# Spreading the d_all transfers over four slots, one product behind the second scan, and a Silu read from PSUM, in a Mamba-then-attention kernel

## The chip, the cores and the metric

The kernel runs on one core of one Trainium2 chip. The metric is device time in microseconds (us) for the whole program, as the median of several runs; three runs of the kernel before gave 7906.63, 7911.72 and 7912.80 us. The trace belongs to one further execution.

## What is computed

The input x is 4 images of 512 channels by 64 x 64 points, float32. Two layers follow each other, each added to its input.

- Layer 0: a group norm over 16 channels, then a layer norm over the 512 channels. The channels are cut into 4 chunks of 128, and each chunk goes through the same Mamba mixer over L = 4096 points: a projection to 2 x 256 (xi and a gate z), a causal convolution with 4 taps on xi, Silu on both, a projection to a time step dt and to B and C of 16 states, and the recurrence

```
h[t] = exp(dt[t] * A) * h[t-1] + dt[t] * x[t] * B[t]      # 256 channels x 16 states
y[t] = sum over states of h[t] * C[t]
out  = out_proj((y + D * x) * silu(z)) + skip * input
```

  Another layer norm and a 512 x 512 projection end the layer.
- Layer 1: a group norm and a linear attention (relu on q and k; k and q are summed over all points first, so that the second half is one 512 x 512 matrix applied to every point).

## The kernel before, in words

**Steps and slots.** The points of an image are cut into tiles of T = 512. A *step* is one image, one tile and one chunk: 4 x 8 x 4 = 128 steps, in that order. Within a step the 256 channels are two halves (e = 0, 1), the 16 states four groups of four (q), and the channels of a half four blocks of 32 (j). One instruction then holds 32 channels x 4 states on the 128 partitions. A *slot* is two of the four blocks of one (e, q); a step has SLOTS = 2 x 4 x 2 = 16 slots, e = 0 in slots 0 to 7 and e = 1 in slots 8 to 15. Two slots, an even one and the odd one after it, are a *pair*: they fill one tile h of four blocks (`hs`, 2 buffers).

**What a slot does** (`slot`, L725). VectorE (DVE) runs two scans (L739), each h of one block from a decay dA in PSUM and an input bx. ScalarE (ACT) makes the decays, dA = exp(dt * A) (`decay`, L713), three ahead (LEAD = 3, three PSUM banks), so a decay can be written only when the scan three before it has read its bank. GpSimd (POOL) makes bx = d * B for two blocks at once (`drive`, L721), two slots ahead with three buffers. In an even slot, between its two scans, the finished pair before it is multiplied by C: the first 384 of 512 points on DVE, with C spread over partitions in a PSUM bank (`product`, L759; `c_row` refills that one bank), while POOL did the last 128 points at the end of the odd slot (L751, C from `c_sb`). TensorE (PE) then sums over the states into y (`fold_states`, L763), which frees the h tile.

**What the queues carry.** All DMAs named here are issued by SyncE (SP), in the order of the code. In an even slot `b_row` issues 4 transfers of 64 KB that spread a row of B over partitions (`b_all`, 3 buffers, L688); in an odd slot `c_tail` issues 4 of 16 KB for `c_sb` (2 buffers, L688), for the pair that starts in the next slot and is multiplied at the end of the one after. `d_all` (2 buffers, one for each half) holds dt and dt * x of one half, spread from rows in HBM: `spread` (L633) issues 8 transfers of 256 KB in one go, in slot 1 for the half of slots 8 to 15 of the same step, and in slot 9 for the half of slots 0 to 7 of the next step. The first decay of a half runs in slot 6 or 14, and the first bx too (slot + 2). Every DMA of this program signals on one of eight semaphores, taken in turn, and waits first until the DMA eight before it has landed; this is what the built program of the kernel shows for each DMA.

**Around it.** The order is written out by hand, since the scheduler is off inside the loop (L1095): `after` (L1109) runs at the end of each slot, first what was put off with `later(n, ...)`, then fixed work by slot number s, then pieces of norms, projection and attention from queues (`ahead`, `late`, `rest`, `light`), as far as a credit of matmul work allows. The fixed work that matters here: at slots 3, 5, 6, 7, 8, 9 a piece of `inputs` for two steps ahead (four pieces of convolution, then pz for e = 0 and e = 1, whose PSUM banks are copied into xz one slot later, L608); at slot 3 softplus between two table loads (L1128, L1130); at slot 4 `to_rows`; at slot 10 Silu of the whole xz, 2048 elements (L1049), and a table load back (L1150). AWAY = (3, 10) names those two slots. At slots 1 and 9 POOL also runs `gate` (L781), at slot 4 dt * x (L628).

Of the kernel before, what the change touches and what calls it, by code (L numbers as in the profile page):

```python
# [14 lines left out]
P = 128  # L15
# [9 lines left out]
def kernel(  # L25
# [553 lines left out]
    def inputs(f, xn, c, nm):  # L579

        xz = f["xz"] = wk.tile([P, 2, NH, T], F32, tag="xz", name=f"xz_{nm}", bufs=3)
        pc = [None] * NH

        def taps(e, ks):
            for k in ks:
                mm(
                    pc[e], w_cv[:, k, e * P : (e + 1) * P], xn[:, c, k : k + T],
                    start=(k == 0), stop=(k == NTAP - 1),
                )

        def take(e):
            nc.scalar.activation(xz[:, 0, e, :], pc[e], AF.Identity, bias=cb[:, e : e + 1])

        for e in range(NH):
            pc[e] = work_bank(f"pc_{nm}_{e}", 0)
            taps(e, range(NTAP // 2))
            yield
            taps(e, range(NTAP // 2, NTAP))
            later(1, lambda e=e: take(e))
            yield  # L600
        for e in range(NH):
            pz = work_bank(f"pz_{nm}_{e}", 0)
            mm(
                pz, w_z[:, e * P : (e + 1) * P], xn[:, c, NTAP - 1 : NTAP - 1 + T],
                start=True, stop=True,
            )

            later(1, lambda e=e, pz=pz: nc.scalar.copy(xz[:, 1, e, :], pz))  # L608
            yield

    def time_banks(f, nm):
# [18 lines left out]
        f["d_rows", v] = d_rows  # L630
        later(1, lambda: nc.sync.dma_start(d_rows, both[:, v]))

    def spread(f, e, nm):  # L633

        d = wk.tile([P, 2, NJ, T], F32, tag="d_all", name=f"d_all_{nm}_{e}")
        for v in range(2):
            src = f["d_rows", v].rearrange("(j i) e t -> i e j t", i=BLK)[:, e]
            for k in range(KS):
                nc.sync.dma_start(d[k * BLK : (k + 1) * BLK, v], src)  # L639
        f["d_all", e] = d  # L640

    def mixers(f, nm):

# [81 lines left out]
    def slot(g, last, after):  # L725
        n, e, q, jj = place(g)
        b, t, c = steps[n]
        if g + 2 < last:
            drive(g + 2)
        if jj == 0:  # L730
            if g + 3 * JJ < last:
                b_row(g + 3 * JJ)
            hs[g // JJ] = wk.tile([P, NJ, T], F32, tag="h", name=f"h_{g}", bufs=2)
        elif g + 1 < last:
            c_tail(g + 1)
        h = hs[g // JJ]
        for i in range(2):
            j = jj * 2 + i
            nc.vector.tensor_tensor_scan(  # L739
                h[:, j, :], dAs.pop(2 * g + i), bxs[g][:, i, :],  # L740
                0.0 if t == 0 else st[:, c, e, q, j : j + 1], ALU.mult, ALU.add,
            )
            if 2 * g + i + LEAD < 2 * last:
                decay(2 * g + i + LEAD)
            if i == 0 and jj == 0 and g:
                product(g - 1)
                fold_states(g - 1, last)
        del bxs[g]
        if jj == JJ - 1:
            nc.gpsimd.tensor_copy(st[:, c, e, q, :], h[:, :, T - 1])  # L750
            nc.gpsimd.tensor_tensor(  # L751
                h[:, :, CUT:], h[:, :, CUT:], bc(c_sb.pop(g // JJ), NJ), ALU.mult
            )
        after()
# [291 lines left out]
        return inputs(fs[n], xn[b, t], c, names[n])  # L1046

    def silu(n):
        nc.scalar.activation(fs[n]["xz"], fs[n]["xz"], AF.Silu)  # L1049

    ahead, late, rest, light = [], [], [], []

# [26 lines left out]
    time_steps(fs[0], names[0])  # L1079
    for v in range(2):  # L1080
        to_rows(fs[0], v, names[0])
    spread(fs[0], 0, names[0])
    for g in range(JJ, 3 * JJ, JJ):
        b_row(g)
    c_row(0)
# [9 lines left out]
    with tc.manual_schedule():  # L1095
        credit, seen, mix, held[0], held_x[0] = 0.0, work["mm"], iter(()), 0, 0
        for n, (b, t, c) in enumerate(steps):
            f, nm = fs[n], names[n]
            before = fs[n - 1] if n else None
            nxt = fs[n + 1] if n + 1 < N else None  # L1100
            front = step_inputs(n + 2) if n + 2 < N else iter(())
            last_mix, mix = mix, mixers(fs[n + 2], names[n + 2]) if n + 2 < N else iter(())
            if c == 0 and (t + 1 < NT or b + 1 < B):
                add_to(ahead, tile_norm(b, t + 1) if t + 1 < NT else tile_norm(b + 1, 0))
            if c == 0 and t == 0 and b + 1 < B:
                add_to(light, input_norm(b + 1))
            assert c != 2 or not ahead
            for s in range(SLOTS):
                def after():  # L1109
                    nonlocal credit, seen  # L1110
                    now[0] = n * SLOTS + s
                    for what in [w for at, w in due if at <= now[0]]:
                        what()
                    due[:] = [d for d in due if d[0] > now[0]]
                    if s == 0 and before is not None:
                        take_y(before, n - 1, 1)
                    if s == SLOTS // 2:
                        take_y(f, n, 0)
                    if s < 2:
                        next(last_mix, None)  # L1120
                    if s == 1:
                        spread(f, 1, nm)
                        if before is not None:
                            gate(before, 1)
                    if s == 2 and nxt is not None:
                        time_banks(nxt, names[n + 1])
                    if s == 3 and nxt is not None:
                        nc.scalar.preload_act_table_set("softplus")  # L1128
                        time_steps(nxt, names[n + 1])
                        nc.scalar.preload_act_table_set("natural_log_exp_and_others")  # L1130
                    if s == 6 and before is not None:
                        pb_, pt_, pc_ = steps[n - 1]
                        with_skip(before, xn[pb_, pt_], pc_)
                        if pc_ == NC - 1:
                            add_to(late, leave(pb_, pt_))
                    if s in (3, 5, 6, 7, 8, 9):
                        next(front, None)
                    if s == 4 and nxt is not None:
                        to_rows(nxt, 0, names[n + 1])
                        to_rows(nxt, 1, names[n + 1])  # L1140
                    if s == 4 and before is not None:
                        pb_, pt_, pc_ = steps[n - 1]
                        out_proj(before, xn[pb_, pt_], pc_, names[n - 1])
                    if s == 9:
                        gate(f, 0)
                        if nxt is not None:
                            spread(nxt, 0, names[n + 1])
                    if s == 10 and n + 2 < N:
                        silu(n + 2)
                        nc.scalar.preload_act_table_set("natural_log_exp_and_others")  # L1150
                    if s >= 12:
                        next(mix, None)
                    may = [
                        what for k, what in ((0, "wide"), (1, "one ahead"), (2, "two ahead"))
                        if any(a - 2 * k <= s <= a - k for a in AWAY) or (k == 2 and s == SLOTS - 1)
                    ]
                    if light and light[0][1] == "wait" or s in AWAY and not any(
                        q and q[0][1] == "wide" for q in (ahead, late)
                    ):
                        one(light)  # L1160

                    limit[0] = 1 if 0 < s < 6 else 2
                    credit = min(credit + 3.5 - (work["mm"] - seen), 2.6)
                    busy = False
                    for queue in (ahead, late, rest):
                        kind = queue[0][1] if queue else None
                        if queue is ahead or kind == "free" or credit > 0 or kind == "more" and not busy:
                            start = work["mm"]
                            one(queue, ANYWHERE if queue is ahead and (c, s) > (1, 4) else may)
                            credit -= work["mm"] - start  # L1170
                            busy = busy or work["mm"] - start > 1
                    seen = work["mm"]

                slot(n * SLOTS + s, N * SLOTS, after)
            fs[n - 1].clear() if n else None
        product(N * SLOTS - 1)
        fold_states(N * SLOTS - 1, N * SLOTS)
        now[0] = None
        for _, what in due:
            what()  # L1180
# [60 lines left out]
```

## Time and profile before

| | |
|---|---|
| median of three runs | 7911.72 us |
| the profiled execution | 7900.44 us |
| its span, first to last instruction | 7898.7 us |
| mean granted TensorE clock | 0.901 |
| first scan starts, last scan ends | 123.2 us, 7424.1 us |
| busy: DVE, POOL, PE, ACT | 6908.9, 6894.4, 6434.6, 5509.8 us |
| bytes moved by DMA | 1265.87 MB |

How to read it. In a row of a group, the columns are: line, engine, operation, output<-inputs, partitions x elements of output and input, number; then busy us, mean ns of one; then the engine's idle time just before these instructions, and who ended most of it. In the list of waits a row says which instruction waited for which, us in total, how many times, and the longest. In a timeline a row gives start and length in us, and in brackets the idle time before it with its releaser. SPq is SP's queue: its rows are DMA issues. From 7424 us on only the rest of the last image's attention is left.

### The profile page before, as it was taken

Reading aid. Unit: us, or ns where it says so; the run is one execution under the profiler, and the core shown is the slowest. Engines: PE = TensorE matmul, PEld = TensorE weight load, DVE = VectorE, ACT = ScalarE, POOL = GpSimd, SP = SyncE. Lnnn points to the kernel's source line nnn. Section 1 sums busy time; section 2 is a strip of 40 time slices with the busy share of each in tenths; the row PEclk is TensorE's granted clock in tenths of the full one; section 3 lists DMA queues with packets and bytes.
Section 4 is the critical chain, followed back from the end, with each engine's and each line's share of the span. In section 5 each row is a group of like instructions: output and inputs, shape, how many; then the busy total and the mean of one; then the engine's idle time right before and its main releaser. Section 6 shows DMA issues by size and latency. Waiting matters only on the chain.

```text
span 7898.7 us, 90490 instructions
## 1 busy us (share of the span) xinstructions
PE 6434.6 (81%) x24834; PEld 2109.1 (27%) x24880; DVE 6908.9 (87%) x5650; ACT 5509.8 (70%) x8329; POOL 6894.4 (87%) x4649
## 2 busy tenths in 40 slices
PE   5676777677789888988788888888788888888599
PEld 1121212112223232322222223322122222322144
DVE  5999999999999999989999999998989999988500
ACT  4677777777777777777777777777777777777421
POOL 4999999999999999989999999999999999999500
PEclk7888888788899999999899999999889999999799
DMA  5676666666776666776766666777666666677402
GB/s 156 167 170 168 159 153 158 161 155 165 171 176 165 161 163 159 182 187 174 170 167 169 171 164 159 175 179 181 164 159 169 158 164 155 156 194 182 102 32 91
DMA packets 829184, 1265.87 MB, mean 160 GB/s; under 512 B 183912, under 2 KB 317560, under 8 KB 816384
## 3 DMA queue, kind: packets, MB, share of 16 engines
q1 hardware_dynamic: 804736, 1222.32, 61.5%
q0 software_dynamic: 16896, 33.56, 2.5%
q10 hardware_dynamic: 7040, 4.20, 0.2%
q8 instruction: 195, 3.19, 0.2%
q14 instruction: 317, 2.60, 0.1%
HBM read 1052.78 MB, written 206.57 MB: 159 GB/s over the span
## 4 chain that ended last, share of the span: by engine, by line
DVE 32%; PE 21%; DMA 13%; ACT 12%; issue 8%; POOL 7%; SPq 6%; POOLq 0%; DVEq 0%; ACTq 0%
DVE h L739 22%; DVE h L759 9%; DMA d_all<-d_rows 7%; PE pq L124 5%; POOL bx L721 5%; ACT dA L713 4%; PE pc L124 4%; SPq L688 3%; PE y L124 3%; PE pr L124 2%; SPq L639 2%; PE po L124 2%; DMA c_sb<-c_rows 2%; ACT xz L1049 2%; DMA b_all<-b_rows 2%
## 5 line engine op out<-in xcount | busy, mean ns | idle before, releaser
L721 POOL TENSOR_TENSOR bx<-d_all,b_all 128x1024 f32<-128x1024 f32 x2048 | 4824.4, 2369 | 157.7 <-DVE h L739 141.3
L739 DVE TENSOR_TENSOR_SCAN h<-dA,st,bx 128x512 f32<-128x512 f32 x3584 | 4358.0, 1264 | 372.5 <-ACT dA L713 164.4
L713 ACT ACTIVATE dA<-d_all,a_t 128x512 f32<-128x512 f32 x4096 | 2754.3, 687 | 1501.3 <-DVE h L739 1444.7
L759 DVE TENSOR_TENSOR h<-h,c_all 128x1536 f32<-128x1536 f32 x1024 | 1767.6, 1726 | 0.1
L751 POOL TENSOR_TENSOR h<-h,c_sb 128x512 f32<-128x512 f32 x1024 | 1301.1, 1271 | 227.2 <-DMA c_sb<-c_rows 125.1
L124 PE MATMUL y<-h,fold 128*32 128x512 f32 x8192 | 1271.6, 697 | 93.2 <-POOL h L751 88.6
L124 PE MATMUL c_all<-parts,sel 128*128 128x384 bf16 x1024 | 368.3, 360 | 1073.2 <-DVE h L759 1071.0
L124 PE MATMUL pc<-xn,w_cv 128*128 128x512 f32 x2048 | 1037.4, 640 | 118.7 <-DVE xn L414 63.9
L124 PE MATMUL pq<-w_qk,xa 128*128 128x512 f32 x2048 | 963.8, 604 | 7.8 <-issue 4.9
L739 DVE TENSOR_TENSOR_SCAN h<-dA,bx 128x512 f32<-128x512 f32 x512 | 591.8, 1204 | 88.5 <-ACT dA L713 62.7
L124 PEld LDWEIGHTS <-sel 128*128 128x128 bf16 x1280 | 126.8, 99 | 1716.1 <-DVE h L759 1519.5
L124 PEld LDWEIGHTS pc<-xn,w_cv 128*128 128x128 f32 x2048 | 386.5, 199 | 736.4 <-issue 418.0
L124 PEld LDWEIGHTS pq<-w_qk,xa 128*128 128x128 f32 x2048 | 396.6, 195 | 443.7 <-issue 425.4
L124 PE MATMUL pr<-xb,m 128*128 128x512 f32 x1024 | 481.8, 608 | 12.3 <-DMA xb<-x 7.0
L124 PE MATMUL pp<-xn,w_pr 128*128 128x512 f32 x1024 | 477.9, 597 | 4.8 <-DVE xn L414 4.8
L124 PEld LDWEIGHTS y<-h,fold 128*32 128x32 f32 x8192 | 170.3, 114 | 661.9 <-issue 322.4
L124 PE MATMUL y<-xz,dg 32*32 32x512 f32 x2048 | 335.8, 731 | 0.0
L781 POOL TENSOR_TENSOR xz<-xz 128x512 f32<-128x512 f32 x256 | 325.9, 1273 | 5.9 <-ACT xz L778 5.8
L832 ACT ACTIVATE kq<-pq 128x512 f32<-128x512 f32 x256 | 150.6, 588 | 253.3 <-PE pq L124 252.5
L124 PE MATMUL pd<-xz,w_xp 128*128 128x512 f32 x512 | 318.3, 753 | 7.8 <-ACT xz L1049 7.8
L628 POOL TENSOR_TENSOR dt<-dt,xz 128x1024 f32<-128x1024 f32 x128 | 302.5, 2363 | 22.5 <-ACT dt L620 22.5
L124 PE MATMUL pz<-xn,w_z 128*128 128x512 f32 x512 | 273.2, 625 | 9.7 <-ACT xz L608 8.2
(177 smaller groups left out, 5981.2 us busy)
## 6 DMA issues: line engine op xcount, KB each, us to landing
d_all<-d_rows SPq DMA_DIRECT2D x2048, 256.0 KB, 6.6
b_all<-b_rows SPq DMA_DIRECT2D x4096, 64.0 KB, 2.2
d_rows<-dt SPq DMA_DIRECT2D x256, 512.0 KB, 3.7
c_sb<-c_rows SPq DMA_DIRECT2D x4096, 16.0 KB, 1.8
xs<-in_x_dram SPq DMA_DIRECT2D x32, 1024.0 KB, 6.1
xn<-in_x_dram SPq DMA_DIRECT2D x32, 1024.0 KB, 6.2
xr<-in_x_dram POOLq DMA_DIRECT2D x32, 1024.0 KB, 10.2
x<-xr SPq DMA_DIRECT2D x32, 1024.0 KB, 4.2
```

Of the source, the lines that this page charges most:

```text
L124: nc.tensor.matmul(out_, lhsT, rhs, **how)
L628: nc.gpsimd.tensor_tensor(f["both"][:, 1], f["both"][:, 0], f["xz"][:, 0], ALU.mult)
L639: nc.sync.dma_start(d[k * BLK : (k + 1) * BLK, v], src)
L688: nc.sync.dma_start(dst[k * BLK : (k + 1) * BLK, :], rows_[q * KS + k, :].partition_broadcast(BLK))
L713: nc.scalar.activation(dAs[k], fs[n]["d_all", e][:, 0, j, :], AF.Exp, scale=a_t[:, e, j, q : q + 1])
L721: nc.gpsimd.tensor_tensor(bxs[g], fs[n]["d_all", e][:, 1, jj * 2 : jj * 2 + 2, :], bc(b_all[g // JJ], 2), ALU.mult)
L739: nc.vector.tensor_tensor_scan(h[:, j, :], dAs.pop(2 * g + i), bxs[g][:, i, :], 0.0 if t == 0 else st[:, c, e, q, j : j + 1], ALU.mult, AL ...
L751: nc.gpsimd.tensor_tensor(h[:, :, CUT:], h[:, :, CUT:], bc(c_sb.pop(g // JJ), NJ), ALU.mult)
L759: nc.vector.tensor_tensor(own, own, bc(c_all.pop(g // JJ), NJ), ALU.mult)
L781: nc.gpsimd.tensor_tensor(f["xz"][:, 1, e, :], f["xz"][:, 1, e, :], f["xz"][:, 0, e, :], ALU.mult)
L832: nc.scalar.activation(qk[i], pq, AF.Relu)
L1049: nc.scalar.activation(fs[n]["xz"], fs[n]["xz"], AF.Silu)
```

## The change

Three edits.

1. `spread` takes a part 0 to 3 and issues 2 of the 8 transfers: parts 0 and 1 are the dt half (v = 0), parts 2 and 3 the dt * x half (v = 1). They run in slots 0 to 3 (was: all in slot 1) and 8 to 11 (was: all in slot 9). The d_all tile is taken with part 0, one slot earlier than before. `gate(before, 1)` stays in slot 1.
2. In slot 10 alone, `product` and `fold_states` of the pair before come behind the second scan (and the decay behind it), not between the two scans.
3. The second half of the gate branch is no longer copied from PSUM to xz and then put through Silu with the rest: Silu of slot 10 becomes one instruction of 1536 elements in place, and one of 512 elements from the PSUM bank pz to xz.

```diff
-            later(1, lambda e=e, pz=pz: nc.scalar.copy(xz[:, 1, e, :], pz))
+            if e + 1 < NH:
+                later(1, lambda e=e, pz=pz: nc.scalar.copy(xz[:, 1, e, :], pz))
+            f["pz"] = pz
             yield
...
-    def spread(f, e, nm):
-        d = wk.tile([P, 2, NJ, T], F32, tag="d_all", name=f"d_all_{nm}_{e}")
-        for v in range(2):
-            src = f["d_rows", v].rearrange("(j i) e t -> i e j t", i=BLK)[:, e]
-            for k in range(KS):
-                nc.sync.dma_start(d[k * BLK : (k + 1) * BLK, v], src)
-        f["d_all", e] = d
+    def spread(f, e, nm, part):
+        if part == 0:
+            f["d_all", e] = wk.tile([P, 2, NJ, T], F32, tag="d_all", name=f"d_all_{nm}_{e}")
+        v, half = divmod(part, 2)
+        src = f["d_rows", v].rearrange("(j i) e t -> i e j t", i=BLK)[:, e]
+        for k in range(half * KS // 2, (half + 1) * KS // 2):
+            nc.sync.dma_start(f["d_all", e][k * BLK : (k + 1) * BLK, v], src)
...
-            if i == 0 and jj == 0 and g:
+            if i == int(g % SLOTS == AWAY[1]) and jj == 0 and g:
                 product(g - 1)
                 fold_states(g - 1, last)
...
     def silu(n):
-        nc.scalar.activation(fs[n]["xz"], fs[n]["xz"], AF.Silu)
+        xz = fs[n]["xz"].rearrange("p i e t -> p (i e) t")
+        nc.scalar.activation(xz[:, : 2 * NH - 1], xz[:, : 2 * NH - 1], AF.Silu)
+        nc.scalar.activation(xz[:, 2 * NH - 1], fs[n]["pz"], AF.Silu)
...
-                    if s == 1:
-                        spread(f, 1, nm)
-                        if before is not None:
-                            gate(before, 1)
+                    if s < 4:
+                        spread(f, 1, nm, s)
+                    if s == 1 and before is not None:
+                        gate(before, 1)
...
                     if s == 9:
                         gate(f, 0)
-                        if nxt is not None:
-                            spread(nxt, 0, names[n + 1])
+                    if 8 <= s < 12 and nxt is not None:
+                        spread(nxt, 0, names[n + 1], s - 8)
```

Ahead of the loop, the first `spread` is called for its four parts one after the other.

More of the change, by code (lines that the diff above doesn't have):

```diff
@@ L1081 @@
         to_rows(fs[0], v, names[0])
-    spread(fs[0], 0, names[0])
+    for part in range(4):
+        spread(fs[0], 0, names[0], part)
     for g in range(JJ, 3 * JJ, JJ):
```

## Prediction

> **What bounds the kernel now.** I read the page's busy times, the list of waits, SP's waits, then the timelines of single steps.
>
> ```profile
> PE 6434.6 (81%) x24834; PEld 2109.1 (27%) x24880; DVE 6908.9 (87%) x5650; ACT 5509.8 (70%) x8329; POOL 6894.4 (87%) x4649
> ```
>
> All scans lie between 123.2 and 7424.1 us: 7301 us for 128 steps, 57.0 us a step. DVE and POOL are both busy some 94% of that. The change gives DVE no instruction and takes none away, so the loop shortens by exactly the idle time that DVE loses. Here is who makes it idle (waiting instruction <- releaser: us in total, times, longest):
>
> ```profile
> DVE h L739 <- ACT dA L713: 227.1, 188, 46.4
> POOL bx L721 <- DVE h L739: 141.3, 228, 3.6
> POOL h L751 <- DMA c_sb<-c_rows: 125.1, 81, 5.7
> DVE h L739 <- PE y L124: 91.6, 87, 4.1
> DVE h L739 <- POOL bx L721: 90.5, 79, 4.6
> ```
>
> No one engine is the bound: DVE waits for decays (227.1, of which 46.4 is the start), for sums on PE, and for POOL; POOL waits for c_sb. I sorted these by place, as a step always has 32 scans. The decay waits lie almost all at the second scan of slot 5 (75.4 us, behind the softplus tables) and of slot 12 (61.5 us, behind Silu). The c_sb waits lie at slots 5 and 13. Why there, SP's own waits tell:
>
> ```profile
> SPq L688 <- DMA d_all<-d_rows: 1573.9, 1737, 2.8
> ```
>
> That is 12.3 us a step. The 8 d_all transfers take all eight semaphores, so the next 8 issues (4 of b_all, 4 of c_sb) each wait until one d_all has landed. In one step SP's queue, and below it POOL, look like this:
>
> ```profile
> 3362.19 4.27 SPq L639 DMA_DIRECT2D d_all<-d_rows  x8
> 3367.62 0.34 SPq L143 DMA_DIRECT2D xb<-x  x1
> 3368.82 4.01 SPq L688 DMA_DIRECT2D b_all<-b_rows  x4
> 3373.70 5.77 SPq L688 DMA_DIRECT2D c_sb<-c_rows  x4
> ```
>
> ```profile
> 3377.28 0.19 POOL L750 COPY st<-h 128x4 f32<-128x4 f32 x1
> 3381.69 1.27 POOL L751 TENSOR_TENSOR h<-h,c_sb 128x512 f32<-128x512 f32 x1 [4.22 <-DMA c_sb<-c_rows]
> ```
>
> Four issues take 1.76 us where nothing is in the way; here 4.01 and 5.77, and POOL stands still for 4.22 us.
>
> **What the Trainium skill says.** "DMA: Bandwidth & Descriptors", section "Anatomy of one DMA", says that DMA engines do not wait on semaphores: a wait happens on the issuing sequencer. The 1573.9 us at SP agree: one late d_all holds up small transfers that have nothing to do with it. "ScalarE: Activation LUTs", section "What ACT_TABLE_LOAD costs", gives about 1283 ns for a load and as much again for a drain. The trace agrees with the load (1.28 us) and shows no drain: copy 0.58, load 1.28, Silu 1.91, load 1.28 make 5.05, and 5.05 us is what lies between the two decays around them in most steps. The same section prices an ACTIVATE at 186 ns + 0.833 ns an element; for 2048 that is 1.89, and the trace has 1.91.
>
> **Edit 1, d_all in four parts.** The same transfers, the same bytes, 16 issues a step at 0.43 us: no issue time is won. In the new order 2 d_all stand in each run of 6 issues. A d_all is waited for 8 issues later: for the first that is the b_row two slots on, which waits for POOL in any case (drive of the slot before), some 4.4 us after issue: b_row and c_tail alternate with POOL's two 2.36 us drives and 1.46 us of st and h. A d_all takes 6.6 us to land (median) with eight in flight, 3.2 at least; with two to four I take 4. So most of 12.3 us of SP wait goes, and with it the c_sb waits that d_all causes. POOL's waits for c_sb come to 139 us (125.1, and 14.2 put down to b_all). I found about 20 us of them behind 1 MB loads of x; these stay. What does DVE gain? Looking back from each DVE wait for bx (99 us by place, those put down to st with them), 54 us have a c_sb wait within the seven slots before; and late POOL multiplies hold back PE's sums, some 12 of the 91.6 us. So 66 us of DVE idle are in reach, of which I take 85%: **56 us**. Bounds: 25 (DVE waits for something else next) and 100 (the other bx waits too, as POOL gets its lead back). Edit 1 also moves the last d_all part two slots later. Slot 11's part is issued behind b_row of slot 10, which follows the drive of slot 9 on POOL: 1.76 + 0.86 + 1.76 + 0.86 = 5.2 us after it. Its user, the drive of slot 14, comes after st and h, gate, four drives and two more st and h: 1.46 + 1.27 + 4 x 2.36 + 2 x 1.46 = 15.1 us. With 6.6 to land that leaves 3.3 us, so I cost it at nothing. The cover is POOL's own queue; if it is gone, each us of lateness is a us of POOL, 256 times.
>
> **Edit 2, the product of slot 10.** DVE's work up to the second scan of slot 12 is the same, so moving it gains only if ACT goes away sooner. ACT's last decay before the tables waits for the bank of slot 10's second scan, and that scan comes 1.73 us earlier. Where ACT waited for it, the gain is up to 1.73; where ACT was late, nothing. Both occur (timelines of ACT):
>
> ```profile
> 3997.31 0.69 ACT L713 ACTIVATE dA<-d_all,a_t 128x512 f32<-128x512 f32 x1 [2.14 <-DVE h L739]
> 3997.94 0.58 ACT L608 COPY xz<-pz 128x512 f32<-128x512 f32 x1
> 3998.54 1.28 ACT L1049 ACT_TABLE_LOAD   x1
> 3999.83 1.91 ACT L1049 ACTIVATE xz<-xz 128x2048 f32<-128x2048 f32 x1
> 4001.76 1.28 ACT L1150 ACT_TABLE_LOAD   x1
> ```
>
> ```profile
> 3016.32 3.63 DVE L739 TENSOR_TENSOR_SCAN h<-dA,st,bx 128x512 f32<-128x512 f32 x3
> 3020.18 1.28 DVE L739 TENSOR_TENSOR_SCAN h<-dA,st,bx 128x512 f32<-128x512 f32 x1 [0.23 <-POOL bx L721]
> 3021.38 1.73 DVE L759 TENSOR_TENSOR h<-h,c_all 128x1536 f32<-128x1536 f32 x1
> 3025.62 2.46 DVE L739 TENSOR_TENSOR_SCAN h<-dA,st,bx 128x512 f32<-128x512 f32 x2 [2.52 <-ACT dA L713]
> ```
>
> In the step at 3025.62 ACT had two pairs of statistics (L561) to do before its decays, so its 2.52 us stay. Step by step, the smaller of DVE's wait and ACT's wait for that scan sums to 35 of the 61.5 us. Against it: product ends one scan (1.25 us) later, PE's c_row and sums with it (2.3 us in slot 10), and the first scan of slot 12 needs the h tile that they free. Where PE came late for other reasons the delay vanishes in that; step by step, delay less slack sums to 11 us. Net **35 - 11 = 24 us**; bounds -15 and 55.
>
> **Edit 3, Silu from PSUM.** Removed: a copy, 0.58, and the 1.91. Added, neither in the trace: by the skill's price, an estimate, 186 + 0.833 x 1536 = 1.47 us and, for 512, 0.61; the trace's copy of 512 from PSUM has 0.58. Sum 2.08 against 2.49: 0.41 us a step, 52 us of ACT, not on the path except where DVE waits behind Silu. There it adds 7 us to the 35 (the same sum with 0.41 more allowed). Slot 13's 6.6 us of decay wait may go too. I take **8 us**. The pz bank is held 1.28 + 1.47 + 0.61 - 0.58 = 2.8 us longer; the next use of it comes two banks later, whose owners ACT reads only after Silu; nothing to 20 us.
>
> **Sum.** 56 + 24 + 8 = 88 us; an idle time that goes leaves PE and softplus relatively later, so I take 80. The profiled run: 7900.44 - 80 = 7820. It lies 11.3 us under the median of the runs shown, so the forecast is 7911.7 - 80, about 7830.
>
> **Rivals.**
> - *All of it passes*: DVE's waits for bx (90), the 43 us behind Silu and 30 of PE's go: 165 us, 7747. For: POOL waits for DVE (141.3) at the very places where DVE waits for decays, so one stall costs both. Against: slot 4's dt * x (2.36) and the gates put POOL behind without any c_sb.
> - *Hidden*: PE, busy for 1533 of 1800 us in a window of the second image, or slot 5's decays take over the waits, or SP still waits as d_all lands in over 4.4 us: 25 us, 7887. For: two steps with 2 us of c_sb wait more or less took the same 55.5 us in the first image.
> - *Late d_all, slower*: a 1 MB load (6.2 us) ahead of a last part makes 6.6 + 6.2 = 12.8 against 9.9 us: 2.9 us late. 168 such transfers lie in 2048 slots; a quarter in the slots of the two last parts, 42, makes 122 us, and the sum 7912 - 80 + 122 = 7954. It decides from 33 late parts on (96 us). Against: the longest landing of any d_all before, loads and all, is 13.5 us with eight in flight, and only some 20 us of the c_sb waits lie behind loads.
>
> **How the numbers follow.** Forecast 50% (7797 to 7862), all passes 15%, hidden 25%, late 10%. A measurement of this kernel tells about 0.2%, 16 us, from no change. Hidden gives 16% faster and 9% within it. Faster 0.81, same 0.09, slower 0.10. The range leaves out the late case and half of the first rival: 7765 to 7895.
>
> **What would show it.** SP's wait for d_all well under 800 us; POOL's for c_sb under 40; DVE's for dA down by some 45, all of it in slot 12; DVE's for PE y up by no more than 15; POOL waiting for d_all nowhere. If POOL's bx waits for d_all, or c_sb waits stay over 90, I am wrong on edit 1; if slot 12 keeps its 61 us, on edits 2 and 3.

## The result, and the profile after

The changed kernel took **7844.13 us** (median of 6 runs, 7834.43 to 7853.48) against 7912.26 (6 runs, 7906.63 to 7915.06) of the kernel before: ratio 0.9917, 95% interval 0.9907 to 0.9928, some 66 us faster. The forecast was 7830 (7765 to 7895). The profiled execution took 7841.65 us, span 7839.9. Most lines are shifted by two: the scan is now L741, product L761, decay L715, drive L723, POOL's h multiply L753.

The page's busy row and then the list of waits of the changed kernel (waiting instruction <- releaser: us, times, longest):

```profile
PE 6444.6 (82%) x24837; PEld 2113.0 (27%) x24880; DVE 6904.3 (88%) x5650; ACT 5457.0 (70%) x8329; POOL 6904.2 (88%) x4649
```

```profile
DVE h L741 <- ACT dA L715: 190.7, 128, 44.5
POOL bx L723 <- DVE h L741: 164.6, 322, 3.0
...
DVE h L741 <- PE y L124: 100.4, 107, 3.0
...
DVE h L741 <- POOL bx L723: 40.5, 42, 3.8
...
POOL h L753 <- DMA c_sb<-c_rows: 21.8, 16, 5.2
```

DVE's busy time is what it was; its idle time fell. Its waits for bx went from 90.5 to 40.5 and for decays from 227.1 to 190.7, and POOL's for c_sb from 125.1 to 21.8. One row rose: DVE's wait for PE's y, from 91.6 to 100.4. SP's own waits, same columns:

```profile
SPq L690 <- POOL st L752: 1111.8, 645, 9.0
SPq L690 <- DMA d_all<-d_rows: 309.6, 541, 2.5
```

SP stands still about as long as before (2714 us over all its waits, 2838 before), but for another reason: 1574 us of waiting for d_all became 310, and 1112 us (235.5 before) now pass in waiting for POOL. That wait does no harm here: SP is ahead of POOL and waits for POOL to get that far, and POOL's own waits for c_sb fell. The step whose queue the prediction showed, SP first and then POOL:

```profile
3347.45 1.71 SPq L690 DMA_DIRECT2D b_all<-b_rows  x4
3349.20 0.91 SPq L642 DMA_DIRECT2D d_all<-d_rows  x2
3350.30 4.21 SPq L690 DMA_DIRECT2D c_sb<-c_rows  x4
3354.55 0.90 SPq L642 DMA_DIRECT2D d_all<-d_rows  x2
3355.62 2.55 SPq L690 DMA_DIRECT2D b_all<-b_rows  x4
3359.24 0.36 SPq L984 DMA_DIRECT2D out_dram<-res  x1
3359.69 1.99 SPq L690 DMA_DIRECT2D c_sb<-c_rows  x4
```

```profile
3362.23 0.19 POOL L752 COPY st<-h 128x4 f32<-128x4 f32 x1
3362.50 1.27 POOL L753 TENSOR_TENSOR h<-h,c_sb 128x512 f32<-128x512 f32 x1
```

The c_sb of slot 13 (the row at 3350.30) was issued well ahead of POOL's multiply, and the 4.22 us in which POOL stood still are gone. ACT's way through Silu in that step:

```profile
3350.80 1.30 ACT L715 ACTIVATE dA<-d_all,a_t 128x512 f32<-128x512 f32 x2
3352.12 1.28 ACT L1052 ACT_TABLE_LOAD   x1
3353.41 1.48 ACT L1052 ACTIVATE xz<-xz 128x1536 f32<-128x1536 f32 x1
3354.80 0.58 ACT L1053 ACTIVATE xz<-pz 128x512 f32<-128x512 f32 x1
3355.40 1.28 ACT L1155 ACT_TABLE_LOAD   x1
```

It is away for 4.62 us, not 5.05. So far all as forecast. What was not forecast stands in slots 10 to 12. Here is DVE in one step (the twentieth) of the kernel before, and then of the changed one:

```profile
1203.08 1.73 DVE L759 TENSOR_TENSOR h<-h,c_all 128x1536 f32<-128x1536 f32 x1
1204.72 3.62 DVE L739 TENSOR_TENSOR_SCAN h<-dA,st,bx 128x512 f32<-128x512 f32 x3
1208.91 1.28 DVE L739 TENSOR_TENSOR_SCAN h<-dA,st,bx 128x512 f32<-128x512 f32 x1 [0.56 <-PE y L124]
1210.11 1.73 DVE L759 TENSOR_TENSOR h<-h,c_all 128x1536 f32<-128x1536 f32 x1
1212.50 1.28 DVE L739 TENSOR_TENSOR_SCAN h<-dA,st,bx 128x512 f32<-128x512 f32 x1 [0.66 <-ACT dA L713]
```

```profile
1201.23 1.73 DVE L761 TENSOR_TENSOR h<-h,c_all 128x1536 f32<-128x1536 f32 x1
1202.88 2.45 DVE L741 TENSOR_TENSOR_SCAN h<-dA,st,bx 128x512 f32<-128x512 f32 x2
1207.48 1.28 DVE L741 TENSOR_TENSOR_SCAN h<-dA,st,bx 128x512 f32<-128x512 f32 x1 [2.15 <-ACT dA L715]
1208.68 1.73 DVE L761 TENSOR_TENSOR h<-h,c_all 128x1536 f32<-128x1536 f32 x1
1210.33 1.28 DVE L741 TENSOR_TENSOR_SCAN h<-dA,st,bx 128x512 f32<-128x512 f32 x1
```

The wait at slot 12's second scan (0.66) is gone, and the one at its first grew from 0.56 to 2.15. The label says ACT; PE in the same stretch of the changed kernel says otherwise:

```profile
1203.02 0.50 PE L124 MATMUL c_all<-parts,sel 128*128 128x384 bf16 x1 [4.26 <-DVE h L761]
1203.45 1.93 PE L124 MATMUL y<-xz,dg 32*32 32x512 f32 x8
1205.31 1.94 PE L124 MATMUL y<-h,fold 128*32 128x512 f32 x8
```

PE begins when the product ends, does c_row and the diagonal (y<-xz,dg) first, and the sums that free the h tile end at 1207.25, just ahead of the scan at 1207.48. So this was a wait for PE, and the list's 100.4 understates it. Over all steps the same holds: of DVE's 83 us at the first scan of slot 12, 78 fall in steps where the sums end less than 0.5 us before the scan starts, and the list has them under four labels (PE y, POOL bx, POOL st, ACT dA). In the kernel before it is 46 of 53.

Below, DVE's idle time by place, summed over all 128 steps from the traces (us), and the times of all kernels. The kernel before had 7916.95, 7914.59 and 7918.06 us in the three groups of runs (labels 1 to 4, 5 to 8, 9 to 12).

| kernel (edits) | median us | ratio, 95% interval | slot 12, 1st scan | slot 12, 2nd scan | slot 10, 2nd scan |
|---|---|---|---|---|---|
| before | 7912.26 | 1 | 53 | 61.5 | 0 |
| e1 (1) | 7868.16 | 0.9938, 0.9925 to 0.9950 | 50 | 64.0 | 0 |
| e2 (2) | 7909.21 | 0.9994, 0.9986 to 1.0003 | 79 | 22.2 | 7 |
| e3 (3) | 7892.49 | 0.9970, 0.9959 to 0.9982 | 52 | 35.8 | 0 |
| e4 (1, 3) | 7819.78 | 0.9881, 0.9868 to 0.9895 | 51 | 36.8 | 0 |
| e12 (1, 3 again) | 7813.00 | 0.9871, 0.9857 to 0.9884 | 52 | 36.7 | 0 |
| e11 (1, 2) | 7847.41 | 0.9919, 0.9907 to 0.9931 | 75 | 22.3 | 7 |
| changed (1, 2, 3) | 7844.13 | 0.9917, 0.9907 to 0.9928 | 83 | 16.6 | 7 |
| e5 (1, 2, 3, diagonal a slot ahead) | 7832.48 | 0.9892, 0.9878 to 0.9905 | 25 | 37.4 | 15 |
| e6 (1, 3, diagonal a slot ahead) | 7853.02 | 0.9921, 0.9908 to 0.9933 | 27 | 69.3 | 0 |
| e7 (1 with four a slot, 3) | 7827.65 | 0.9885, 0.9870 to 0.9900 | 51 | 37.2 | 0 |
| e8 (1 one slot later, 3) | 7862.23 | 0.9930, 0.9918 to 0.9943 | 53 | 35.5 | 0 |
| e9 (1, 2, 3, diagonal between the scans) | 7797.97 | 0.9856, 0.9842 to 0.9869 | 50 | 18.4 | 7 |
| e10 (as e9, c_row behind the sums) | 7800.15 | 0.9858, 0.9843 to 0.9873 | 39 | 19.6 | 7 |

### The profile page after: what moved, and what is told of

Read it like the earlier page. It is cut to its first block, busy times and chain, and to the rows that moved or that the text cites. A ratio compares the mean times of both kernels' runs of the same rounds, so it can differ in the third digit from the quotient of the medians.

```text
span 7839.9 us, 90362 instructions
## 1 busy us (share of the span) xinstructions
PE 6444.6 (82%) x24837; PEld 2113.0 (27%) x24880; DVE 6904.3 (88%) x5650; ACT 5457.0 (70%) x8329; POOL 6904.2 (88%) x4649
## 4 chain that ended last, share of the span: by engine, by line
DVE 33%; PE 31%; ACT 11%; DMA 8%; issue 7%; POOL 6%; SPq 3%; POOLq 0%; DVEq 0%; ACTq 0%
DVE h L741 21%; DVE h L761 10%; PE y L124 6%; PE pc L124 6%; PE pq L124 5%; POOL bx L723 4%; ACT dA L715 4%; DMA d_all<-d_rows 3%; PE pr L124 3%; PE po L124 3%; PE pp L124 2%; SPq L690 2%; DMA c_sb<-c_rows 2%; PE c_all L124 1%; DMA b_all<-b_rows 1%
## 5 line engine op out<-in xcount | busy, mean ns | idle before, releaser
L723 POOL TENSOR_TENSOR bx<-d_all,b_all 128x1024 f32<-128x1024 f32 x2048 | 4829.5, 2369 | 184.7 <-DVE h L741 164.6
L741 DVE TENSOR_TENSOR_SCAN h<-dA,st,bx 128x512 f32<-128x512 f32 x3584 | 4360.0, 1269 | 317.0 <-ACT dA L715 132.8
L715 ACT ACTIVATE dA<-d_all,a_t 128x512 f32<-128x512 f32 x4096 | 2758.2, 687 | 1491.7 <-DVE h L741 1435.2
L761 DVE TENSOR_TENSOR h<-h,c_all 128x1536 f32<-128x1536 f32 x1024 | 1772.4, 1731 | 0.1
L753 POOL TENSOR_TENSOR h<-h,c_sb 128x512 f32<-128x512 f32 x1024 | 1301.4, 1271 | 108.2 <-DMA c_sb<-c_rows 21.8
L741 DVE TENSOR_TENSOR_SCAN h<-dA,bx 128x512 f32<-128x512 f32 x512 | 590.6, 1206 | 80.7 <-ACT dA L715 57.9
L124 PE MATMUL y<-xz,dg 32*32 32x512 f32 x2048 | 358.9, 778 | 0.0
```

What stands on the lines that cost most here:

```text
L124: nc.tensor.matmul(out_, lhsT, rhs, **how)
L715: nc.scalar.activation(dAs[k], fs[n]["d_all", e][:, 0, j, :], AF.Exp, scale=a_t[:, e, j, q : q + 1])
L723: nc.gpsimd.tensor_tensor(bxs[g], fs[n]["d_all", e][:, 1, jj * 2 : jj * 2 + 2, :], bc(b_all[g // JJ], 2), ALU.mult)
L741: nc.vector.tensor_tensor_scan(h[:, j, :], dAs.pop(2 * g + i), bxs[g][:, i, :], 0.0 if t == 0 else st[:, c, e, q, j : j + 1], ALU.mult, AL ...
L753: nc.gpsimd.tensor_tensor(h[:, :, CUT:], h[:, :, CUT:], bc(c_sb.pop(g // JJ), NJ), ALU.mult)
L761: nc.vector.tensor_tensor(own, own, bc(c_all.pop(g // JJ), NJ), ALU.mult)
```

## The experiments

My theory on reading the result: edit 1 does its work through the semaphores, edits 2 and 3 both shorten the wait behind Silu, and edit 2 pays for it at PE. The rivals: each edit contributes its forecast share and all fall a little short; or edit 1's gain is one of contention among the DMAs.

### One edit at a time

**e1, edit 1 alone**: the kernel before with the `spread` edit and its calls only.

> Edit 1 alone: d_all's transfers two a slot, product and Silu as before. My theory, the semaphore ring: SP's wait for d_all falls from 1574 to about 310 us and POOL's wait for c_sb from 139 (b_all's label with it) to about 25, as in the changed kernel, and that alone is worth about 45 us, 7867, two thirds of the 68 that the whole change gave. Rival A, c_sb is hidden (DVE waits for something else in its place): under 15 us. Rival B, all the gain is from here: 65 us or more, 7847.

**e2, edit 2 alone**:

```diff
-            if i == 0 and jj == 0 and g:
+            if i == int(g % SLOTS == AWAY[1]) and jj == 0 and g:
```

> Edit 2 alone: in slot 10 the product behind the second scan. The forecast had 35 us won at the second scan of slot 12 and 11 lost at its first scan: about 24 us, 7888. The trace of the changed kernel shows more lost there (the first scan of slot 12 waits for PE's sums, some 25 us more than before), so I now expect 10 us, 7902. Rival: the loss is a matter of the other edits, and 24 us are there. If it comes out slower than before, the product's place costs more on PE than it frees on ACT.

**e3, edit 3 alone**: the `pz` and `silu` edits only.

> Edit 3 alone: the second half of the gate branch through Silu from PSUM, without its copy. It takes 0.43 us out of ACT's absence (0.58 + 1.91 against 1.48 + 0.58), and by the step-by-step sum of the trace before at most 25 us of DVE's waits behind Silu with it: 15 to 20 us, 7895. Rival, DVE's waits behind Silu go on as POOL or PE ends them: nothing, 7912.

**e4, edits 1 and 3**: the changed kernel with `if i == 0` back in `slot`.

> Edits 1 and 3 without 2. If edit 2 is worth what the forecast said on top of the others (24 us less what edit 3 takes already, some 17), this is 7861, 17 us slower than the changed kernel's 7844. If its gain and its loss on PE are about equal, this is within 8 us of the changed kernel: 7844 to 7852. DVE's wait at the second scan of slot 12 should be about 37 us here (61 less 25) against 17 in the changed kernel, its wait at the first scan about 50 against 83.

Measured, by the ratios: e1 -49 us, e2 -5 with an interval that holds no change, e3 -24, e4 -94. SP's wait in e1:

```profile
SPq L688 <- DMA d_all<-d_rows: 330.6, 601, 2.9
```

Edit 1 alone gives nearly the whole fall of SP's wait for d_all. Edit 2 alone does what it was meant to at the second scan of slot 12 (61.5 to 22.2 us) and gives it back at the first (53 to 79) and in a new place, the second scan of slot 10, which now comes before the product and finds its decay not ready (7 us). And e4 is faster than the changed kernel, with intervals apart (0.9868 to 0.9895 against 0.9907 to 0.9928): **on top of edits 1 and 3, edit 2 costs some 28 us**. Neither of the two answers set down for e4 (17 us over the changed kernel, or within 8 us of it) had that, and the rival that each edit gives its share and falls a little short is out. Edits 1 and 3 together give more than their sum (94 against 49 + 24). The traces say where most of the surplus lies. DVE's idle time in the loop was 451.1 us before, 408.5 in e1, 448.5 in e3 and 374.6 in e4. In e3 alone DVE's wait for bx rose from 90.5 to 117.0, with POOL still held up by c_sb (144.5), so that nearly all that ACT gave was lost there; in e4 it is 49.9, as in e1 (47.7). One caution: the 24 us of e3 stand in the medians, not in this pair of traces, whose runs took 7900.44 and 7896.06 us. The profiled run of the kernel before is faster than every other run of it (7903.24 at least).

### The order on PE

**e5 and e6**: the changed kernel, and e4, with the diagonal one slot ahead (in the two pairs of a step that open a y bank) and `c_row` behind the sums (in every pair).

```diff
+            if i == 1 and jj == 1 and q == 0:
+                ys[n, e] = ps_y.tile([P, T], F32, tag="y", name=f"y_{n}_{e}")
+                diagonal(ys[n, e], dg[:, e, :], fs[n]["xz"][:, 0, e, :])
...
     def fold_states(g, last):
-        if g + 1 < last:
-            c_row(g + 1)
-        if q == 0:
-            ys[n, e] = ps_y.tile([P, T], F32, tag="y", name=f"y_{n}_{e}")
-            diagonal(ys[n, e], dg[:, e, :], fs[n]["xz"][:, 0, e, :])
...
+        if g + 1 < last:
+            c_row(g + 1)
```

> All three edits, and the diagonal matmuls that open a y bank (8 of about 0.22 us) are issued one slot ahead, in the odd slot, and c_row behind the sums over states instead of ahead of them. Theory (edit 2 costs time because the product ends 1.25 us later and PE then puts c_row 0.45 and the diagonal 1.75 to 1.94 us ahead of the sums that free the h tile): the sums end some 2.2 us sooner, the first scan of slot 12 no longer waits for them (DVE's wait for PE y from 100 to about 60 us, the wait in slot 12's first scan from 83 to about 45), and the time falls by 25 to 40 us, to about 7815. Rival (the loss of edit 2 is the longer way through ACT, or POOL's bx): within 8 us of 7844.

> Edits 1 and 3 alone, with the diagonal matmuls one slot ahead and c_row behind the sums. Theory (PE's latency from product to freed h tile is on DVE's path wherever DVE waits for PE y, 75 us in edits 1 and 3): the 2.2 us of the two pairs per step that open a bank go, DVE's wait for PE y to about 45, time down by 10 to 30 us, to about 7800. Rival (those waits come from PE's other work, attention and norms, ahead of the sums): within 8 us of 7820. If this one and the kernel with all three edits and the same reordering come out alike, edit 2 is worth nothing even when its price is gone; if the latter is lower, the gain of 35 us forecast for it exists.

Measured: 7832.48 (20 us under the changed kernel by the ratios) and 7853.02. The wait at the first scan of slot 12 fell as the theory wanted (83 to 25, and 51 to 27), but the list's whole wait for PE's y rose, where it was to fall: to 113.0 in e5 (from 100.4) and 121.8 in e6 (from 75.2 in e4). And e6 is slower than e4 by 32 us, which neither side expected. In e6 the second scan of slot 12 waits 69.3 us, 33 more than in e4, where the first waits 24 less; in slot 5 DVE is idle for 111 us in all (91 in e4). The reordering touched every pair and two slots at once, so it says that the first scan waits for PE, and nothing on edit 2's price. I did not find out which of the two moves does the harm. The mean granted clock of their runs, 0.894 and 0.892, is the lowest of all kernels here (0.898 to 0.906 in the others); whether that is part of the loss was not tested.

**e9 and e10**: the changed kernel, touched in slot 10 alone. e9 issues the diagonal between the two scans and leaves product, c_row and sums behind the second, so that on PE the diagonal now comes ahead of all that needs the product (in the kernel before it came behind the product and c_row); e10 also puts `c_row` behind the sums there.

```diff
+            if i == 0 and g % SLOTS == AWAY[1]:
+                first_y(g - 1)
             if i == int(g % SLOTS == AWAY[1]) and jj == 0 and g:
                 product(g - 1)
                 fold_states(g - 1, last)
...
+    def first_y(g):
+        n, e, _, _ = place(g)
+        ys[n, e] = ps_y.tile([P, T], F32, tag="y", name=f"y_{n}_{e}")
+        diagonal(ys[n, e], dg[:, e, :], fs[n]["xz"][:, 0, e, :])
...
-        if q == 0:
-            ys[n, e] = ps_y.tile([P, T], F32, tag="y", name=f"y_{n}_{e}")
-            diagonal(ys[n, e], dg[:, e, :], fs[n]["xz"][:, 0, e, :])
+        if q == 0 and (n, e) not in ys:
+            first_y(g)
```

> All three edits, and in slot 10 alone the 8 diagonal matmuls that open the y bank are issued between the two scans, where they stood before edit 2, so that PE runs them under the second scan and the product; c_row and the sums stay behind the product. Everything else is as in the kernel with all three edits. Theory (edit 2's loss is PE's way from the product's end to the freed h tile, of which the diagonal is 1.75 to 1.94 of some 4.3 us): the wait at slot 12's first scan falls from 83 to 35 to 50 us, and the time by about 30 us against the kernel with all three edits (7844), to about 7815. That the reordering in every opening of a bank gave only 12 us would then be the diagonal in slots 1 and 9 itself, in the way of other PE work. Rival (the first scan of slot 12 is late for another reason, or another wait takes the place): within 10 us of 7840.

> As the one with the diagonal first, and in slot 10 c_row goes behind the sums, not ahead of them: 0.35 to 0.45 us less on the way to the freed h tile, and c_row's bank is filled some 2 us later, which the product of slot 12 needs only 4 us on. Theory: the wait at slot 12's first scan falls by another 5 to 20 us; time 5 to 15 us under the one with the diagonal first, about 7805. Rival (PE's order costs elsewhere): no lower than the one with the diagonal first.

e9: 7797.97, 0.9856 (0.9842 to 0.9869): 48 us under the changed kernel, by the ratios, intervals apart. In the twentieth step, PE and DVE of e9:

```profile
1193.78 1.06 PE L124 MATMUL y<-xz,dg 32*32 32x512 f32 x8
1198.13 0.32 PE L124 MATMUL c_all<-parts,sel 128*128 128x384 bf16 x1 [3.30 <-DVE h L763]
1198.39 1.30 PE L124 MATMUL y<-h,fold 128*32 128x512 f32 x8
```

```profile
1196.36 1.73 DVE L763 TENSOR_TENSOR h<-h,c_all 128x1536 f32<-128x1536 f32 x1
1198.00 3.62 DVE L741 TENSOR_TENSOR_SCAN h<-dA,st,bx 128x512 f32<-128x512 f32 x3
1201.55 1.72 DVE L763 TENSOR_TENSOR h<-h,c_all 128x1536 f32<-128x1536 f32 x1
```

The diagonal (PE's first row) is done before the wait for the product, the sums end 1.6 us after the product instead of 4.3, and the scans run through (x3: the first scan of slot 12 is the third). For the product of slot 10, the mean over all steps from its end to the end of the sums is 3.48 us before, 3.24 in the changed kernel, 2.29 in e9, 2.06 in e10. The list of waits of e9:

```profile
DVE h L741 <- PE y L124: 65.7, 83, 2.6
```

It was 100.4. The wait at slot 12's first scan went from 83 to 50, that of its second stayed low (16.6 and 18.4). Between the two profiled runs DVE's idle time in the loop fell by 37 us (397 to 360), 33 of them at that first scan. This is the theory's answer: what edit 2 loses, it loses on PE's way from the product to the h tile. The granted clock does not explain the gain: its mean is 0.898 in the changed kernel and 0.899 in e10, which is 47 us faster by the ratios. e10 cut the first scan's wait by 11 us more than e9, but its time is that of e9: the expected 5 to 15 us did not show.

One rival stands. The diagonal stood behind the product in the kernel before too, so e9 does not give back what edit 2 took; it takes out of the way something that was always in it. Edits 1 and 3 with the diagonal between the scans in slot 10 alone were not run, so how much of e9's time needs edit 2 is open. A third h buffer was not tried.

**e11**, e1 with edit 2, and **e12**, e4 once more beside e9 and e10:

> Edits 1 and 2 without edit 3. Theory (edit 2 loses about 39 us at slot 12's first scan and slot 10's second in any company, and wins at slot 12's second scan what edit 3 has not already taken: 39 us without it, 20 with it): within 10 us of edit 1 alone, 7868; the wait at slot 12's second scan 20 to 25 us, at its first about 80. Rival (the loss comes with edit 1, as POOL is now earlier and PE's lateness shows more): 20 us or more over edit 1 alone.

> Edits 1 and 3 once more, on the chip of these runs, as the one to beat: 7820 within 8 us. The theory puts the two with the diagonal first at or below it, since their second scan in slot 12 waits 20 us less; the rival puts them over it.

e11 came out at 7847.41: 0.9919 against 0.9938 of e1, overlapping intervals and a point 15 us lower. So edit 2 loses nothing where edit 3 is absent, and the rival falls; the gain of 15 us is somewhat more than the 10 within which the theory put it. The waits bear the theory out: with edit 2 the first scan loses 25 to 32 us in any company, but the second wins 42 without edit 3 (64.0 to 22.3) and only 20 with it (36.8 to 16.6). Read the other way, edit 3 on top of 1 and 2 gives nothing (0.9919, 0.9917). e9 lies 12 us under e12 by the ratios, with overlapping intervals: it beats both kernels of this study clearly, but edits 1 and 3 alone only probably.

### How far d_all may be spread, and how late

**e7**: e4 with parts 0 and 1 in slots 1 and 9, parts 2 and 3 in slots 2 and 10. **e8**: e4 with all parts one slot later.

```diff
-                    if s < 4:
-                        spread(f, 1, nm, s)
+                    if 1 <= s < 5:
+                        spread(f, 1, nm, s - 1)
...
-                    if 8 <= s < 12 and nxt is not None:
-                        spread(nxt, 0, names[n + 1], s - 8)
+                    if 9 <= s < 13 and nxt is not None:
+                        spread(nxt, 0, names[n + 1], s - 9)
```

> Edits 1 and 3 with d_all issued four a slot over two slots (1 and 2, 9 and 10) instead of two over four. Theory (the order of semaphores alone: an issue waits for the DMA eight before it, so with four d_all in a run of eight half as many small transfers stand behind one that was issued just before): SP's wait for d_all between 330 and 1574 us, about 700; POOL's wait for c_sb about 50; time between 7820 and 7892, about 7840. Rival (what counts is that d_all and the small transfers don't share the DMA engines at once): c_sb waits fall as far as with two a slot, time within 8 us of 7820.

> Edits 1 and 3 with all four parts of d_all one slot later (slots 1 to 4 and 9 to 12): the test of the rival of a late d_all. The working of the prediction left a margin of 3.3 us with a landing of 6.6 us, and a slot is 3.5 us; with the 4.4 us of landing that the trace of the changed kernel shows, the margin is 5.5 us. If the working is right: POOL waits for d_all for less than 20 us in all, the time stays within 10 us of 7820. If the margin was only the 3.3 us or less: POOL's bx waits for d_all some tenths of a us in most steps, at two places a step, 50 us or more, and the time is over 7860.

e7, SP's waits and then POOL's:

```profile
SPq L690 <- DMA d_all<-d_rows: 650.4, 859, 1.9
```

```profile
POOL h L753 <- DMA b_all<-b_rows: 27.6, 20, 6.3
POOL h L753 <- DMA c_sb<-c_rows: 22.9, 14, 5.9
```

The small transfers' wait for d_all is 650 us and POOL's for c_sb 50 (with what is put down to b_all), both where the theory put them, but the time is that of two a slot (0.9885 against 0.9881 and 0.9871). By the time alone that was the rival's number; the waits speak for the theory, with a limit: below some 50 us of POOL's wait, less of it was worth nothing that these runs can measure. A d_all also landed sooner the fewer stood in a run (6.6, 5.8 and 4.4 us with eight, four and two), and no run separates that from the order of the semaphores. e8 is slower than e4 by 39 to 47 us (by the ratios to e4 and e12). Its POOL:

```profile
POOL bx L723 <- DMA d_all<-d_rows: 49.6, 20, 5.6
POOL bx L723 <- DMA c_sb<-c_rows: 29.7, 17, 5.3
```

bx reads no c_sb, so the second row is put down to the wrong transfer. Ahead of the two drives that first use d_all (run in slots 6 and 14) POOL is idle for 98 us, against 7 in e4; over the whole loop its idle time rose by 48, from 333 to 380. Of the two answers set down this is the second: one slot later, d_all comes too late in part of the steps.

## Why the prediction was right, and where it was wrong

- **Edit 1, forecast 56: right, 49 measured (e1).** By the forecast's own signs, in the changed kernel: SP's wait for d_all 310 (under 800), POOL's for c_sb 22 and 3 put down to b_all (under 40), POOL's for d_all 1.8 us in all. A d_all lands in 4.4 us (4 taken; 6.6 before). The way to DVE was the one foretold, mostly through bx: in e1 DVE's wait for bx fell from 90.5 to 47.7 (54 were put in reach), and that for PE's y by 4 (12). The Trainium skill's "DMA: Bandwidth & Descriptors", section "Anatomy of one DMA", that a wait happens on the issuing sequencer and not in a DMA engine, is what this rested on (its heading names the GpSimd path; these transfers are SyncE's), and e1 agrees: the same bytes in another order took 1243 us of waiting for d_all out of SP's queue.
- **Edit 2, forecast 24: wrong, and this is the step that failed.** The gain was sized rightly: 35 us at the second scan of slot 12, 39 measured alone (e2). The loss was not: "step by step, delay less slack sums to 11 us" came out as 25 at the first scan of slot 12, and 7 more in slot 10 that the working did not have. Alone that makes a wash, and on top of edits 1 and 3, where the second scan has only 20 to give, a loss. Too much was made of "where PE came late for other reasons the delay vanishes in that". PE did come late: in the trace of before it reached c_row more than 1.25 us after the product's end in 50 of 128 steps. But in e2 the sums ended on average only 0.27 us sooner after the product than before, so that some 0.9 us of the delay reached the h tile. In the median step of before the sums end 0.8 us before DVE is ready for the first scan of slot 12, in e2 just as it is ready, and DVE waits there in 71 steps instead of 51. Why PE's lateness took up so little of the delay is not shown. Nor did the working ask which of PE's work needs the product: the diagonal stood behind it and does not need it (e9).
- **Edit 3, forecast 8: right in kind, too small: 24 alone (e3).** The price was right: 1.48 and 0.58 us, against 1.47 and 0.61 estimated by the Trainium skill's "ScalarE: Activation LUTs", section "What ACT_TABLE_LOAD costs". The term was counted as what edit 2 leaves over. Counted alone, the smaller of each step's wait at that scan and 0.43 us sums to 26 us in the trace of before; e3 took 26 off (61.5 to 35.8), though in its trace DVE lost as much waiting for bx; with edit 1 in place (e1 to e4) it kept it, and the time fell by 45.
- **The sum, 88 cut to 80, came to 66 to 68.** Edits 2 and 3 were added as if they took different idle time; they take the same. Their order in the sum decided which looked worthless: I gave the overlap to edit 2, which pays for it, and left edit 3 with the rest, which has it for nothing. That the whole came so near is in part luck: edits 1 and 3 gave 94 us where 64 were forecast, and edit 2 took 28 where it was to give 24.
- **The signs.** DVE's wait for decays fell by 36, not 45. Under that label slot 12's second scan gave 43 and other places 24 (slot 15 most, 8.5), but slots 5 and 10 took 11 and 7, and slot 12's first scan 13, which are PE's. DVE's wait for PE's y rose by 9 in the list (no more than 15 was the sign); by the end of the sums, DVE waits for PE 32 us more at slot 12's first scan alone (46 to 78): over it.
- **The rivals.** "All of it passes" (its parts, 90, 43 and 30, make 163, not 165) and "hidden" are out by the time. "Late d_all" named a mechanism that exists: at the place chosen it doesn't act, one slot on it costs 39 to 47 us (e8). The margin that I put at 3.3 us with a landing of 6.6 would be 5.5 with the landing that was measured; e8, with a slot of 3.5, shows that this is too much for a part of the steps. "Each us of lateness is a us of POOL" is too much: of 91 us that POOL stood longer ahead of these drives, about half stayed, in its idle time (48) as in the time of the kernel.

## What to carry to other kernels

Where several edits go after the same wait, size each alone and then the set, and prefer those that pay nothing for it. Before a producer is moved later, list in issue order all that stands behind it on the next engine: what doesn't need it can go ahead (here eight matmuls, 48 us). Large transfers that shared semaphores with small ones were worth interleaving with them here (49 us), and how late they may come is measured by moving them one slot on.

## What the runs showed of the hardware that was not expected

The median c_sb transfer of 16 KB took 1.8 us from issue to landing in the kernel before, 2.0 with d_all four in a run (e7), and 3.6 with two d_all in front of it (the changed kernel). Yet POOL's waits for c_sb went the other way: 139, 50 and 25 us. Issued early enough, a transfer that lands later cost less here. d_all itself landed in 6.6, 5.8 and 4.4 us.
